# A state-space scan in double steps: first states by copies, evictions moved, and two additions given to TensorE

## The chip, the cores and the metric

The kernel runs on one core of one Trainium2 chip. The metric is the device time of one execution in microseconds (us), taken as the median of several runs. Three runs of the kernel before took 3832.01, 3835.03 and 3840.7 us. A profile is one further execution, with its own time. Its engines are called PE (TensorE's matmuls; PEld its weight loads), DVE (VectorE), ACT (ScalarE), POOL (GpSimd) and SP (SyncE, which issues most DMAs).

## What is computed

Four residual layers on an input of 3 images, 256 channels and 48 x 48 points, each `x = x + layer(groupnorm(x))`: an attention block, two convolutions, and a state-space scan. Only the last layer is touched by the change. Cut to what matters, for a sequence of 2304 points:

```python
xn = (xf - mean(xf)) * rsqrt(var(xf) + 1e-5) * norm_w + norm_b   # over 256 channels
x_in, z = split(xn @ in_proj_w.T)                                # 512 channels each
u = silu(causal_conv4(x_in) + conv_b)
dt_raw, B, C = split(u @ x_proj_w.T)                             # 16, 16, 16
dt = softplus(dt_raw @ dt_proj_w.T + dt_proj_b)                  # 512 channels
h = h * exp(dt * A) + dt * B * u                                 # 512 x 16 states, point by point
y = sum_n(h * C) + u * D
out = (y * silu(z)) @ out_proj_w.T
```

## The kernel before, in words

The first three layers fill the first 2,200 us or so; they are the same in both kernels. The scan layer (from line 995) cuts each image into 6 chunks of 384 points (`CH`), 18 chunks in all, taken one after the other. The 512 channels are four groups `m` of 128, and the 16 states of a channel four groups `g` of 4. A step `s = (chunk, m, g)` covers 128 channels times 4 states times 384 points. It is laid out as 128 partitions (32 channels times 4 states) by 4 rows `q` of 384 points, in a tile `hs`. There are 16 steps a chunk, 288 in all, and `j = 4m + g` numbers them in the chunk. A step consists of:

- `fill` (L1285): `hs = dt*u*B`. DVE multiplies rows 0 and 1 (L1291; the factor comes from PSUM, where PE spread it in `spread_pe`, L1268), POOL rows 2 and 3 (L1292; the factor comes by DMA, `spread`, L1258). The fill of step s+1 is written ahead of step s's scans.
- `decay` (L1296): ACT writes `exp(dt*A)` of one row into one of three PSUM tiles `ps_da` (L1304), three rows ahead of the scan.
- four scans on DVE (L1360), one for each row, along the 384 points. The first state is the constant 0 in an image's first chunk, else a column of `hst`, a pointer to 128 values, which ACT copied from the chunk before (L1372).
- the product with C on POOL (L1375), into `hc`.
- `add_states` (L1309), two steps later: PE adds the states, four small matmuls (L1320), into `ps_y`, in the first step of an `m` behind a diagonal matmul for `u*D` (L1316).
- `gate` (L1325): DVE multiplies the finished `ps_y` by silu(z) (L1327), six steps after the first step of its `m`.

`hs` has four buffers and `hc` three. All other work of the layer is written into the same steps from three lists (`plan`, `after`, `gating`): each entry has a `j`, a place and a chunk relative to the running one. MID is after the second scan of the step, LATE after its product, PE_ after LATE and `add_states`. So chunk k+2 gets its group norm and layer norm (group_scale, two `channel_mean`s on PE, `centre`, `inverse_root`, `normalise`, `tokens`), and chunk k+1 its convolution (`taps`, four times 16 matmul instructions), `take_u`, silu, `project_u`, `take_dbc`, `project_dt`, `softplus`, `take_dt` and `project_z`. The chunk before gets `project_y` and `store`. A silu needs an ACT table of its own and loads the old one again behind it. All these use one PSUM tile `bank` of two banks in turn, so the next user of a bank waits for the last reader.

The order in which lines are written is the order on each of PE, DVE, ACT and POOL: `keep_order` (L1397) chains every instruction to the one before it on its engine. An instruction that waits therefore holds up all that are written after it on the same engine. SP's queue takes its DMAs in the written order as well.

Of the kernel before, what the change touches and what calls it, by code (L numbers as in the profile page):

```python
# [9 lines left out]
F32 = mybir.dt.float32  # L10
I32 = mybir.dt.int32
AF = mybir.ActivationFunctionType
ALU = mybir.AluOpType
# [69 lines left out]
def net(  # L83
# [908 lines left out]

    with ExitStack() as l3:
        wp = l3.enter_context(tc.tile_pool(name="w3", bufs=1))
        act = l3.enter_context(tc.tile_pool(name="act", bufs=2))
        scn = l3.enter_context(tc.tile_pool(name="scn", bufs=2))
        psd = l3.enter_context(tc.tile_pool(name="psd", bufs=3, space=PSUM))
        psr = l3.enter_context(tc.tile_pool(name="psr", bufs=1, space=PSUM))  # L1000
        psg = l3.enter_context(tc.tile_pool(name="psg", bufs=1, space=PSUM))
        psy = l3.enter_context(tc.tile_pool(name="psy", bufs=1, space=PSUM))
# [32 lines left out]
            )  # L1035
        fold = rep[:, 0, :]

        diag = wp.tile([P, DI, P], F32, name="diag")
        for m in range(DI):
            nc.vector.tensor_scalar(diag[:, m, :], ident, v("D", m), None, ALU.mult)  # L1040
# [23 lines left out]
                    bias=sh[:, ct : ct + 1], scale=sc[:, ct : ct + 1],  # L1064
                )

        def channel_mean(src, j):
            for ct in range(CT):
                nc.tensor.matmul(  # L1069
                    bank[:, j, :CH], mean2, src[:, ct, :], start=ct == 0, stop=ct == CT - 1  # L1070
                )

        def centre(k):
            mu = bank[:, 0, :CH].unsqueeze(1).broadcast_to([P, CT, CH])
            nc.vector.tensor_tensor(k.xg, k.xg, mu, ALU.subtract)
            k.sq = act.tile([P, CT, CH], F32, name="sq", bufs=1)
            nc.scalar.activation(k.sq, k.xg, AF.Square)

# [23 lines left out]
        def taps(k, m, lo, hi):  # L1102
            for tap in range(lo, hi):
                for ct in range(CT):
                    nc.tensor.matmul(  # L1105
                        bank[:, m % 2, :CH], wtap[:, tap, ct, m * P : (m + 1) * P],
                        k.xn[:, ct, tap : tap + CH],
                        start=tap == 0 and ct == 0, stop=tap == DCONV - 1 and ct == CT - 1,
                    )

        def take_u(k, m):
            nc.scalar.activation(  # L1112
                k.u[:, m, :], bank[:, m % 2, :CH], AF.Identity, bias=v("conv_b", m)
            )
# [46 lines left out]
        def take_dt(k, m0):  # L1161
            both, pdt = k.dt[:, m0 : m0 + 2, :], bank[:, :, :CH]
            nc.vector.scalar_tensor_tensor(pdt, pdt, 0.0, both, ALU.max, ALU.add)
            nc.vector.tensor_tensor(
                k.dtu[:, m0 : m0 + 2, :], pdt, k.u[:, m0 : m0 + 2, :], ALU.mult
            )
            nc.scalar.copy(both, pdt)  # L1167
            if m0 == 2:
                k.dtd = dram.tile([P, DI, CH], F32, name="dtd")
                nc.sync.dma_start(k.dtd, k.dt)  # L1170
                k.dtud = dram.tile([P // 2, DI, CH], F32, name="dtud")
                nc.sync.dma_start(k.dtud, k.dtu[P // 2 :])
# [13 lines left out]
        def project_y(k, mo):  # L1186
            for m in range(DI):
                nc.tensor.matmul(  # L1188
                    bank[:, mo, :CH], w("out", m * 256 + mo * P, P), k.sz[:, m, :],
                    start=m == 0, stop=m == DI - 1,  # L1190
                )

        def residual(k):
            k.ot = act.tile([P, CT, CH], F32, name="ot")
            nc.sync.dma_start(k.ot, xd[k.b][:, :, k.c * CH : (k.c + 1) * CH])

        def store(k, mo):
            o = k.ot[:, mo, :]
            nc.vector.tensor_tensor(o, bank[:, mo, :CH], o, ALU.add)  # L1199
            nc.sync.dma_start(  # L1200
                out[k.b, mo * P : (mo + 1) * P, k.c * CH : (k.c + 1) * CH], o
            )

        MID, LATE, PE_ = range(3)
        plan = [
            (12, MID, 2, group_scale),
            (12, PE_, 2, lambda k: channel_mean(k.xg, 0)),
            (13, MID, 2, centre),  # L1210
            (13, PE_, 2, lambda k: channel_mean(k.sq, 1)),
            (14, MID, 2, inverse_root),
            (14, LATE, 2, normalise),
            (15, MID, 2, tokens),
            (0, PE_, 1, lambda k: taps(k, 0, 0, 4)),
            (1, LATE, 1, lambda k: take_u(k, 0)),
            (1, PE_, 1, lambda k: taps(k, 1, 0, 4)),
            (3, MID, 1, lambda k: take_u(k, 1)),
            (3, PE_, 1, lambda k: taps(k, 2, 0, 4)),
            (4, PE_, 1, lambda k: taps(k, 3, 0, 4)),  # L1220
# [3 lines left out]
            (7, PE_, 1, project_u),  # L1224
            (8, LATE, 1, take_dbc),
            (8, PE_, 1, lambda k: project_dt(k, 0)),
            (9, MID, 1, lambda k: softplus(k, 0)),
            (10, MID, 1, lambda k: take_dt(k, 0)),
            (10, PE_, 1, lambda k: project_dt(k, 2)),
            (11, MID, 1, lambda k: softplus(k, 2)),  # L1230
            (12, MID, 1, lambda k: take_dt(k, 2)),
        ]

        after = [
# [2 lines left out]
            (4, MID, -1, residual),  # L1237
            (6, PE_, -1, lambda k: project_y(k, 0)),
            (6, PE_, -1, lambda k: project_y(k, 1)),
            (7, LATE, -1, lambda k: store(k, 0)),  # L1240
            (7, LATE, -1, lambda k: store(k, 1)),
        ]

        gating = [
# [32 lines left out]
            k.ps = t  # L1277


        steps = [(at, m, g) for at in range(len(todo)) for m in range(DI) for g in range(4)]  # L1280
        chunks = {}
        tiles = {}
        state = {}

        def fill(s):  # L1285

            at, m, g = steps[s]
            k = chunks[at]
            bb = k.bc[0][:, g, :].unsqueeze(1).broadcast_to([P, 2, CH])
            hs = tiles[s] = scn.tile([P, 4, CH], F32, name="hs", bufs=4)  # L1290
            nc.vector.tensor_tensor(hs[:, 0:2, :], k.ps[:, :, :CH], bb, ALU.mult)  # L1291
            nc.gpsimd.tensor_tensor(hs[:, 2:4, :], k.rows[m][1], bb, ALU.mult)  # L1292

        decays = []

        def decay(n):  # L1296

            s, q = divmod(n, 4)
            if s >= len(steps):
                return  # L1300
            at, m, g = steps[s]
            da = psd.tile([P, 512], F32, tag="d", name="ps_da")
            col = (m * 4 + g) * 4 + q
            nc.scalar.activation(  # L1304
                da[:, :CH], chunks[at].rows[m][0][:, q, :], AF.Exp, scale=amat[:, col : col + 1]
            )
            decays.append(da)

        def add_states(s):  # L1309

            at, m, g = steps[s]
            k = chunks[at]
            hc = tiles.pop(s)
            if g == 0:
                k.y_ps = psy.tile([P, 512], F32, name="ps_y")
                nc.tensor.matmul(  # L1316
                    k.y_ps[:, :CH], diag[:, m, :], k.u[:, m, :], start=True, stop=False
                )
            for q in range(4):
                nc.tensor.matmul(  # L1320
                    k.y_ps[32 * q : 32 * q + 32, :CH], fold, hc[:, q, :],
                    start=False, stop=g == 3,
                )

        def gate(at, m):  # L1325
            k = chunks[at]
# [9 lines left out]
            stage(k)  # L1336
        k.rows = {0: spread(k, 0)}
        spread_pe(k, 0)
        fill(0)
        for n in range(3):  # L1340
            decay(n)
# [3 lines left out]
        for _, _, _, stage in gating:  # L1345
            stage(k)

        for s, (at, m, g) in enumerate(steps):
            k = chunks[at]
            j = 4 * m + g  # L1350
            if j == 2 and at + 2 <= last:
                fetch(at + 2)
            if s + 1 < len(steps):
                fill(s + 1)

            if g == 2 and s + 2 < len(steps):
                spread_pe(chunks[steps[s + 2][0]], steps[s + 2][1])
            hs = tiles[s]
            for q in range(4):
                nc.vector.tensor_tensor_scan(  # L1360
                    hs[:, q, :], decays[q][:, :CH], hs[:, q, :],
                    0.0 if k.c == 0 else state[m, g][:, q : q + 1], ALU.mult, ALU.add,
                )
                decay(4 * s + q + 3)
                if q == 1:
                    if g == 2 and s >= 6:
                        gate(*steps[s - 6][:2])
                    run(at, j, MID)
            del decays[:4]
            if k.c < NCH - 1:  # L1370
                h = state[m, g] = wp.tile([P, 4], F32, name=f"hst{m}{g}")
                nc.scalar.copy(h.unsqueeze(2), hs[:, :, CH - 1 : CH])  # L1372
            cb = k.bc[1][:, g, :].unsqueeze(1).broadcast_to([P, 4, CH])
            hc = tiles[s] = scn.tile([P, 4, CH], F32, name="hc", bufs=3)
            nc.gpsimd.tensor_tensor(hc, hs, cb, ALU.mult)  # L1375
            run(at, j, LATE)
            if s >= 2:
                add_states(s - 2)
            run(at, j, PE_)
            if g == 1 and m + 1 < DI:  # L1380
                k.rows[m + 1] = spread(k, m + 1)
            elif g == 1 and at < last:
                chunks[at + 1].rows = {0: spread(chunks[at + 1], 0)}
        end = len(steps) - 1
        add_states(end - 1)
        add_states(end)
        gate(*steps[end][:2])
        k = chunks[last]
        residual(k)
        for mo in range(2):  # L1390
            project_y(k, mo)
        for mo in range(2):
            store(k, mo)
        keep_order(tc, listed, mark)


# [110 lines left out]
```

## Time and profile before

| | us |
|---|---|
| median of 3 runs | 3835.03 |
| the profiled execution | 3840.89 |
| its span, first to last instruction | 3839.1 |
| PE busy | 3232.1 (84%) |
| DVE busy | 3221.5 (84%) |
| ACT busy | 2228.0 (58%) |
| POOL busy | 1554.8 (40%) |

The shares are over the whole span. POOL works almost only in the scan layer: the page's slices show it at 0 to 3 tenths up to slice 23 and at 9 from there on. Rows of groups read: line, engine, operation, output<-inputs, shapes, count, then busy us and mean ns of one, then the engine's idle us just before them and what ended most of it. A mean can be longer than the pitch at which instructions start, where one begins before the last has ended. Timeline rows read: start and length in us, engine, line, operation, tiles, how many were merged, and in brackets the idle time before and who ended it.

### The profile page before, as it was taken

Reading aid. Unit: us, or ns where it says so; the run is one execution under the profiler, and the core shown is the slowest. Engines: PE = TensorE matmul, PEld = TensorE weight load, DVE = VectorE, ACT = ScalarE, POOL = GpSimd, SP = SyncE. Lnnn points to the kernel's source line nnn. Section 1 sums busy time; section 2 is a strip of 40 time slices with the busy share of each in tenths; the row PEclk is TensorE's granted clock in tenths of the full one; section 3 lists DMA queues with packets and bytes.
Section 4 is the critical chain, followed back from the end, with each engine's and each line's share of the span. In section 5 each row is a group of like instructions: output and inputs, shape, how many; then the busy total and the mean of one; then the engine's idle time right before and its main releaser. Section 6 shows DMA issues by size and latency. Waiting matters only on the chain. (4 is left out here: it accounts for less than half of the span.)

```text
span 3839.1 us, 45642 instructions
## 1 busy us (share of the span) xinstructions
PE 3232.1 (84%) x17010; PEld 1406.6 (37%) x17010; DVE 3221.5 (84%) x3518; ACT 2228.0 (58%) x3216; POOL 1554.8 (40%) x674
## 2 busy tenths in 40 slices
PE   7999999999999988677699757777878878777874
PEld 4323232432323234355577523333333333333331
DVE  4898989779899963799988349999999999999997
ACT  2788787668878762210000147666677666667763
POOL 0000000000000002100000039999999999999998
PEclk9999999999999999888899878888888888888886
DMA  4000000000000015555101133434443433343441
GB/s 170 3 1 1 1 2 1 26 13 1 1 1 2 1 57 173 174 177 177 45 25 42 59 71 100 105 99 104 103 104 91 108 91 99 100 112 92 111 100 34
DMA packets 149962, 266.50 MB, mean 69 GB/s; under 512 B 23441, under 2 KB 123601, under 8 KB 147170
## 3 DMA queue, kind: packets, MB, share of 16 engines
q1 hardware_dynamic: 137634, 245.80, 22.9%
q10 hardware_dynamic: 12096, 17.70, 1.4%
q8 instruction: 135, 2.21, 0.2%
q14 instruction: 97, 0.79, 0.1%
HBM read 216.31 MB, written 46.89 MB: 69 GB/s over the span
## 5 line engine op out<-in xcount | busy, mean ns | idle before, releaser
L587 ACT ACTIVATE pt<-ps_s 128x1024 f32<-128x1024 f32 x972 | 939.0, 1022 | 237.3 <-PE ps_s L583 219.9
L1375 POOL TENSOR_TENSOR hc<-hs,bc 128x1536 f32<-128x1536 f32 x288 | 991.4, 3443 | 85.6 <-DVE hs L1360 56.7
L663 DVE TENSOR_TENSOR part<-part,pt 128x2048 f32<-128x2048 f32 x396 | 906.6, 2289 | 78.4 <-ACT pt L587 53.8
L1360 DVE TENSOR_TENSOR_SCAN hs<-ps_da,hst,hs 128x384 f32<-128x384 f32 x960 | 909.8, 997 | 23.5 <-ACT ps_da L1304 19.9
L1304 ACT ACTIVATE ps_da<-dtr,amat 128x384 f32<-128x384 f32 x1152 | 657.1, 581 | 359.0 <-DVE hs L1360 339.9
L160 POOL TENSOR_TENSOR rstd<-ve,mhalf 128x2 f32<-128x2 f32 (+1 forms) x26 | 17.5, 675 | 1661.7 <-DVE ve L158 1661.7
L583 PE MATMUL ps_s<-q,kt 32*128 32x512 f32 (+1 forms) x4320 | 616.4, 595 | 2.3 <-DVE q L544 0.9
L1292 POOL TENSOR_TENSOR hs<-dtur,bc 128x768 f32<-128x768 f32 x288 | 523.8, 1819 | 77.5 <-DMA dtr<-dtd 77.5
L596 PE MATMUL acc<-pt,vt 128*32 128x512 f32 (+1 forms) x4320 | 523.5, 563 | 8.2 <-DVE o L643 8.0
L927 PE MATMUL ps_c<-vt,u 128*128 128x288 f32 x1728 | 437.8, 417 | 92.9 <-DVE u L257 55.1
L1105 PE MATMUL ps_g<-xn,wtap 128*128 128x384 f32 x1152 | 392.2, 493 | 36.3 <-ACT u L1112 31.3
L927 PEld LDWEIGHTS ps_c<-vt,u 128*128 128x128 f32 x1728 | 335.4, 195 | 190.0 <-issue 56.3
L583 PEld LDWEIGHTS ps_s<-q,kt 32*128 32x128 f32 x4320 | 220.2, 184 | 389.6 <-issue 230.0
L1320 PE MATMUL ps_y<-hc,rep 128*32 128x384 f32 x2304 | 293.5, 596 | 34.6 <-POOL hc L1375 32.7
L1291 DVE TENSOR_TENSOR hs<-ps_r,bc 128x768 f32<-128x768 f32 x288 | 269.1, 934 | 61.8 <-PE ps_r L1273 61.8
L1105 PEld LDWEIGHTS ps_g<-xn,wtap 128*128 128x128 f32 x1152 | 212.7, 189 | 220.1 <-ACT u L1112 54.9
L596 PEld LDWEIGHTS acc<-pt,vt 128*32 128x32 f32 x4320 | 95.7, 108 | 364.3 <-issue 328.5
L943 ACT COPY cb<-ps_c 128x288 f32<-128x288 f32 x48 | 19.0, 395 | 355.5 <-PE ps_c L927 258.5
L1360 DVE TENSOR_TENSOR_SCAN hs<-ps_da,hs 128x384 f32<-128x384 f32 x192 | 170.7, 937 | 17.9 <-ACT ps_da L1304 17.7
L1176 PE MATMUL ps_g<-xn,w3sb 128*128 128x384 f32 x288 | 133.8, 608 | 58.1 <-ACT sz L1184 43.3
L1069 PE MATMUL ps_g<-xg,mean 128*128 128x384 f32 x72 | 52.7, 887 | 105.3 <-ACT dt L1167 78.2
L1320 PEld LDWEIGHTS ps_y<-hc,rep 128*32 128x32 f32 x2304 | 51.3, 118 | 239.1 <-POOL hc L1375 113.5
(204 smaller groups left out, 3265.5 us busy)
## 6 DMA issues: line engine op xcount, KB each, us to landing
wconv<-in_we SPq DMA_DIRECT2D x144, 384.0 KB, 4.3
dtr<-dtd SPq DMA_DIRECT2D x288, 192.0 KB, 3.6
bc<-bcd SPq DMA_DIRECT2D x144, 192.0 KB, 5.9
dtur<-dtud SPq DMA_DIRECT2D x288, 96.0 KB, 2.7
dtd<-dt SPq DMA_DIRECT2D x18, 768.0 KB, 3.5
yc<-ycat ACTq DMA_DIRECT2D x18, 576.0 KB, 5.3
xb<-in_x SPq DMA_DIRECT2D x6, 1152.0 KB, 11.1
ycat<-cur SPq DMA_DIRECT2D x6, 1152.0 KB, 4.9
```

The lines of the kernel that those rows point to most:

```text
L583: nc.tensor.matmul(s[:, j, cols], kt[r, mt * P : (mt + 1) * P], q[r, :n], start=True, stop=True,)
L587: nc.scalar.activation(p[:, h0 : h0 + 2, :], s, AF.Exp)
L596: nc.tensor.matmul(acc[h * HD : (h + 1) * HD, :n], vt[:, mt, g * P + h * HD : g * P + (h + 1) * HD], p[:, h, cols], start=mt == 0, stop=mt ...
L663: nc.vector.tensor_tensor(part, first_p if group == 1 else part, p, ALU.add)
L927: nc.tensor.matmul(pc[:, :HN], u[:, i, dy, ct, m * P : (m + 1) * P], vt[:, i, ct, dy * TW : dy * TW + HN], start=ct == 0 and dy == 0, stop ...
L1105: nc.tensor.matmul(bank[:, m % 2, :CH], wtap[:, tap, ct, m * P : (m + 1) * P], k.xn[:, ct, tap : tap + CH], start=tap == 0 and ct == 0, st ...
L1291: nc.vector.tensor_tensor(hs[:, 0:2, :], k.ps[:, :, :CH], bb, ALU.mult)
L1292: nc.gpsimd.tensor_tensor(hs[:, 2:4, :], k.rows[m][1], bb, ALU.mult)
L1304: nc.scalar.activation(da[:, :CH], chunks[at].rows[m][0][:, q, :], AF.Exp, scale=amat[:, col : col + 1])
L1320: nc.tensor.matmul(k.y_ps[32 * q : 32 * q + 32, :CH], fold, hc[:, q, :], start=False, stop=g == 3,)
L1360: nc.vector.tensor_tensor_scan(hs[:, q, :], decays[q][:, :CH], hs[:, q, :], 0.0 if k.c == 0 else state[m, g][:, q : q + 1], ALU.mult, ALU.add,
L1375: nc.gpsimd.tensor_tensor(hc, hs, cb, ALU.mult)
```

## The change

- A step becomes a double step `(chunk, m, h)`: two groups `g` at once, eight rows of 384 points. There are 8 a chunk, 144 in all, and places `j` 4m+2h and 4m+2h+1 fall in one of them. MID runs after the second and the sixth scan, LATE after the fourth and the eighth, PE_ of an even `j` after the fourth scan, PE_ of an odd `j` at the end, ahead of `add_states`. The latter now belongs to one double step earlier.
- Every row of `hs` gets one more column, its first, with the first state. `first_states` has ACT copy it (8 columns) before the fills of that step are written; `ps_da` has a zero in that column. Every scan now runs over 385 points with the constant 0 as its first state. Scans go over the rows that DVE filled first, then over POOL's.
- Fills and products are one instruction each for a double step (1536 and 3072 elements a partition). `hs` and `hc` have two buffers.
- `take_u` of the first group goes from LATE of 1 to MID of 2, softplus from MID to LATE of 9 and 11. The copy of dt, with the DMAs behind it, is split off `take_dt` as `keep_dt` and goes to LATE of 10 and 12.
- The layer norm's mean is subtracted by PE: `less_mean` multiplies by identity minus mean (4 matmuls for 2), and `centre` becomes an ACT copy out of PSUM, in LATE. The residual is added by PE with an identity matmul in `project_y`, and `store` becomes one ACT copy in place of two DVE additions.

```diff
-        psd = l3.enter_context(tc.tile_pool(name="psd", bufs=3, space=PSUM))
+        psd = l3.enter_context(tc.tile_pool(name="psd", bufs=1, space=PSUM))
...
+        def less_mean(k):
+            for to in range(CT):
+                for ct in range(CT):
+                    nc.tensor.matmul(
+                        bank[:, to, :CH], less[:, int(to != ct), :], k.xg[:, ct, :],
+                        start=ct == 0, stop=ct == CT - 1,
+                    )
...
         def centre(k):
-            mu = bank[:, 0, :CH].unsqueeze(1).broadcast_to([P, CT, CH])
-            nc.vector.tensor_tensor(k.xg, k.xg, mu, ALU.subtract)
+            nc.scalar.copy(k.xg, bank[:, :, :CH])
             k.sq = act.tile([P, CT, CH], F32, name="sq", bufs=1)
             nc.scalar.activation(k.sq, k.xg, AF.Square)
...
-            nc.scalar.copy(both, pdt)
+
+        def keep_dt(k, m0):
+            nc.scalar.copy(k.dt[:, m0 : m0 + 2, :], bank[:, :, :CH])
...
-                    start=m == 0, stop=m == DI - 1,
+                    start=m == 0, stop=False,
                 )
+            nc.tensor.matmul(bank[:, mo, :CH], ident, k.ot[:, mo, :], start=False, stop=True)
...
-            nc.vector.tensor_tensor(o, bank[:, mo, :CH], o, ALU.add)
...
+            nc.scalar.copy(k.ot, bank[:, :, :CH])
...
-            (13, MID, 2, centre),
-            (13, PE_, 2, lambda k: channel_mean(k.sq, 1)),
+            (13, LATE, 2, centre),
+            (13, PE_, 2, square_mean),
...
-            (1, LATE, 1, lambda k: take_u(k, 0)),
             (1, PE_, 1, lambda k: taps(k, 1, 0, 4)),
+            (2, MID, 1, lambda k: take_u(k, 0)),
...
-            (9, MID, 1, lambda k: softplus(k, 0)),
+            (9, LATE, 1, lambda k: softplus(k, 0)),
             (10, MID, 1, lambda k: take_dt(k, 0)),
+            (10, LATE, 1, lambda k: keep_dt(k, 0)),
             (10, PE_, 1, lambda k: project_dt(k, 2)),
-            (11, MID, 1, lambda k: softplus(k, 2)),
+            (11, LATE, 1, lambda k: softplus(k, 2)),
             (12, MID, 1, lambda k: take_dt(k, 2)),
+            (12, LATE, 1, lambda k: keep_dt(k, 2)),
...
-        steps = [(at, m, g) for at in range(len(todo)) for m in range(DI) for g in range(4)]
+        steps = [(at, m, h) for at in range(len(todo)) for m in range(DI) for h in range(2)]
...
+        parts_of_step = [(g, q) for a in range(2) for g in range(2) for q in (2 * a, 2 * a + 1)]
+        slots = [psd.tile([P, 512], F32, name=f"ps_da{i}") for i in range(3)]
...
+        def first_states(s):
+            at, m, h = steps[s]
+            src = zero if chunks[at].c == 0 else state[m, h]
+            hs = tiles[s] = scn.tile([P, 2, 4, CH + 1], F32, name="hs")
+            nc.scalar.copy(hs[:, :, :, 0], src.rearrange("p (g q) -> p g q", g=2))
...
+        def scan(s, part):
+            g, q = parts_of_step[part]
+            b = tiles[s][:, g, q, :]
+            nc.vector.tensor_tensor_scan(
+                b, slots[(8 * s + part) % 3][:, : CH + 1], b, 0.0, ALU.mult, ALU.add
+            )
...
+            for part in range(8):
+                j = 4 * m + 2 * h + part // 4
+                scan(s, part)
+                decay(8 * s + part + 3)
+                if part % 4 == 1:
+                    if h == 1 and part == 1 and s >= 3:
+                        gate(*steps[s - 3][:2])
+                    run(at, j, MID)
+                if part % 4 == 3:
+                    run(at, j, LATE)
+                if part == 3:
+                    run(at, j, PE_)
...
             if s + 1 < len(steps):
+                first_states(s + 1)
                 fill(s + 1)
+            last_states(s)
+            times_c(s)
+            run(at, 4 * m + 2 * h + 1, PE_)
+            if s >= 1:
+                add_states(s - 1)
+
+            if h == 0 and s + 2 < len(steps):
                 spread_pe(chunks[steps[s + 2][0]], steps[s + 2][1])
```

## The prediction

> **What bounds the kernel now.** I read the page's engine shares and slices first, then the stretch of the scan layer alone, then its costliest groups, then each engine's timeline.
>
> The busy time of each engine in 1,300 us inside the scan layer (slices 24 to 39 of the page):
>
> ```profile
> core 0: us, PE busy (x) PEld busy (x) DVE busy (x) ACT busy (x) POOL busy (x), PEclk, DMA share, GB/s
> 2400.00:3700.00 1300.00, 1039.12 (x4072) 430.50 (x4072) 1202.12 (x1378) 899.55 (x1612) 1242.19 (x482) 0.85 0.40 100
> ```
>
> POOL is busy 95.6% and DVE 92.5%: two engines are nearly full, and each idles only where it waits for another. How long a chunk takes is seen in one instruction that runs once a chunk, with its first and last start at the end of the row:
>
> ```profile
> L1117 ACT ACTIVATE sz<-sz x18: 1483/1483/1485, 2278.3 to 3751.8; 128x1536 f32<-128x1536 f32 x18
> ```
>
> (3751.8 - 2278.3) / 17 = **86.7 us a chunk**. The groups that fill it:
>
> ```profile
> L1375 POOL TENSOR_TENSOR hc<-hs,bc 128x1536 f32<-128x1536 f32 x288 | 991.4, 3443 | 85.6 <-DVE hs L1360 56.7
> ...
> L1360 DVE TENSOR_TENSOR_SCAN hs<-ps_da,hst,hs 128x384 f32<-128x384 f32 x960 | 909.8, 997 | 23.5 <-ACT ps_da L1304 19.9
> ...
> L1291 DVE TENSOR_TENSOR hs<-ps_r,bc 128x768 f32<-128x768 f32 x288 | 269.1, 934 | 61.8 <-PE ps_r L1273 61.8
> ...
> L1360 DVE TENSOR_TENSOR_SCAN hs<-ps_da,hs 128x384 f32<-128x384 f32 x192 | 170.7, 937 | 17.9 <-ACT ps_da L1304 17.7
> ```
>
> POOL's idle time is put down to DVE's scans; DVE's largest is a wait for PE. POOL's timeline gives pitches, start to start, that durations do not:
>
> ```profile
> 2980.55 3.44 POOL L1375 TENSOR_TENSOR hc<-hs,bc 128x1536 f32<-128x1536 f32 x1 [0.61 <-DVE hs L1360]
> 2983.94 1.83 POOL L1292 TENSOR_TENSOR hs<-dtur,bc 128x768 f32<-128x768 f32 x1
> 2985.72 3.44 POOL L1375 TENSOR_TENSOR hc<-hs,bc 128x1536 f32<-128x1536 f32 x1
> ```
>
> 1536 elements take 3.39 us of POOL, 768 take 1.78: 2.1 ns an element and about 0.17 us an instruction.
>
> **The engines' own work after the change, one chunk of eight double steps.** I write (m,h) for the step.
>
> POOL: products of 3072 elements, 3.39 + 1536 x 2.1 ns = 6.6 us, and fills of 1536, 3.4 us; 8 x 10.0 = 80.0 us against 16 x 5.17 = 82.7. The trace shows no POOL instruction whose rows are 385 apart and start at an odd element. The fill's and the product's different shapes share one slope, so I take that. A gain below it is excluded, as the elements are the same; above, the farthest row is VectorE's: 694 ns for a strided 128x288 update (L955) against 458 for a plain one (L945), a factor of 1.5.
>
> DVE: the scan whose first state is a constant starts every 0.85 to 0.86 us (937 ns of duration, overlapping), the one with a pointer every 0.91. All become constant, with a 385th element of 2 ns: 64 x 0.86 = 55.0. A fill of 1536: 0.84 (pitch of 768) plus 768 x 1.04 ns (from 934 less the 536 of the 128x384 product at L1327) = 1.64, at most twice 0.84; 8 x 1.64 = 13.1. Gates 4 x 0.5, take_dt 2 x 1.85, normalise 0.9: 6.6. The centring (0.93) and two residual adds (1.1) go to ACT. Together **74.7 us** of DVE, against 81 before.
>
> So the work alone asks 80. It does not set the chunk, because waits that had been hidden are put in DVE's way.
>
> **Where DVE will wait.** Before a scan may start, `first_states` of its step must have run on ACT, which works in order. That copy (0.18 us, the row of `hst`) is queued behind every ACT operation of LATE at odd places and behind the three exponentials ahead. From the start of a step's last scan, an undisturbed ACT needs 0.98 (scan ends, signal) + 0.58 (exp) + 0.18 + 0.05 = 1.8 us; DVE needs 0.86 + 1.64 = 2.5. Hidden, with 0.7 to spare. What is added to ACT beyond that stops DVE:
>
> - softplus, now at the end of steps (2,0) and (2,1): 2.48 us (89.4 us of L1157 to L1159 over 36). 4.27 against 2.5: **1.8 twice**. Before, it lay mid-step, under three exponentials of reserve.
> - the second silu in (1,1), and the new eviction behind it. Its ACT timeline, for the other silu:
>
> ```profile
> 2971.34 1.28 ACT L1117 ACT_TABLE_LOAD   x1
> 2972.63 1.48 ACT L1117 ACTIVATE sz<-sz 128x1536 f32<-128x1536 f32 x1
> 2974.13 1.28 ACT L223 ACT_TABLE_LOAD   x1
> 2975.43 1.09 ACT L1304 ACTIVATE ps_da<-dtr,amat 128x384 f32<-128x384 f32 x2
> ```
>
>  Load, silu and load back take 4.09 us, and what follows starts at once. From scan 5's start ACT needs 0.98 + 0.58 + 4.09 + 1.09 (two exps) + 0.80 (store's copy, the 128x768 copy of L1184) + 0.23 = 7.8; DVE needs 3 x 0.86 + 1.64 = 4.2. **3.6.** The Trainium skill's page "ScalarE: Activation LUTs", section "What ACT_TABLE_LOAD costs", speaks harder against this place: 1.28 us for a load and 1.38 of drain at every switch. By that rule the wait would be 6.3 and not 3.6; the row above, with 1.29 us from load to activation, decides.
> - centre, at the end of (3,0), waits for PE. From scan 3: 0.98 + 0.58 + 0.80 (keep_dt) + 3.0 (less_mean, eight instructions at 0.34, the pitch of taps, and a start) + 0.80 (copy) + 0.84 (Square) + 0.23 and signals = 7.3; DVE 5 x 0.86 + 1.64 = 5.9. **1.4.** (Rows of four such instructions last 1.56 or 2.93 us, so less_mean lies between 2.9 and 5.9.)
> - tokens (1.57) and take_z (0.47) in (3,1): **0.7.**
>
> Then PE. Every second step's `add_states` moves behind the PE_ stage of its place; before, it came ahead of it. Gate needs it. PE's timeline:
>
> ```profile
> 3066.87 5.43 PE L1105 MATMUL ps_g<-xn,wtap 128*128 128x384 f32 x16 [1.74 <-ACT u L1112]
> 3072.23 0.85 PE L1320 MATMUL ps_y<-hc,rep 128*32 128x384 f32 x8
> 3073.01 5.43 PE L1105 MATMUL ps_g<-xn,wtap 128*128 128x384 f32 x16
> 3078.37 0.85 PE L1320 MATMUL ps_y<-hc,rep 128*32 128x384 f32 x8
> ```
>
> Here additions of 0.8 us lie between two tap sets of 5.4. After the change both tap sets come first:
>
> - the previous chunk's last gate, in (0,1): from the end of take_z(1) PE runs project_z 2 and 3 (2.85), the additions of (3,0) with their diagonal (2.3), two tap sets (10.7), the additions of (3,1) (1.5): 17.4 with signals. DVE comes there after 1.09 + 0.23 + 8 x 0.86 + 1.64 + 2 x 0.86 = 11.6. **5.9.** The first silu costs (0,1) 2.9 us of exponentials and is hidden behind this wait. If the gate were ready, 2.9 would stand here.
> - the gate in (3,1) stands behind square_mean (1.56), project_z 0 (1.45) and 1.5 of additions, all after Square: 4.65 against DVE's 1.95. **2.7.**
>
> Sum: 3.6 + 3.6 + 1.4 + 0.7 + 5.9 + 2.7 = **17.9 us**. 74.7 + 17.9 = **92.6 us a chunk**, 5.9 over 86.7. POOL does not hold DVE in this: with 10.0 us a step it ends each product before the step after next is filled (narrowest between (1,0) and (2,0), under 1 us). Unpriced, because covered: the first copies for zeros; take_u, half a step later (PE works from the other bank); 36 identity matmuls for the residual (under the silu); the DMAs of dtd and dtud, which leave half a step later and have some 11 us until the first exponential of the next chunk, where write (3.5), read (3.6) and eight issues (0.43 each) need 10.6. That last cover is thin; without it each us late is a us.
>
> **Ends.** Fifteen full chunks: 15 x 5.9 = 89. A longer first step +4, chunk 0 (no gate before it) -0.5, chunk 16 +1, the last chunk on POOL's pace -2.5, the tail (copies, identity) +1.5. The profiled execution took 3840.9 us (span 3839.1): 3840.9 + 92 = 3933. It lies 5.9 over the median of the runs (3835.0), so **3927** for the median.
>
> **Rivals.**
> 1. *The other side: POOL keeps the pace.* If the waits come to under 80.0 - 74.7 = 5.3 us a chunk, they vanish in DVE's slack and POOL sets 80.0: 15 x (80.0 - 86.7) = -100, **3735**. For it: POOL is the fullest engine and its idle time is DVE's fault. Against: the two gate waits alone hold 8.6, and each is a queue order in the code with a measured 5.4 behind it. Break-even with today is 12.0 us of waits; half of my list would do for faster.
> 2. *Some waits overlap*, and 12 remain: no change, **3835**.
> 3. *POOL pays for rows of 385.* Beyond a factor of 92.6/80.0 = 1.16 it sets the chunk; at 1.2, 96 us, **3980**; at 1.5, 120 us, over 4300, far from the nearest rows. The skill's "GPSIMD Engine Reference", section "Performance pitfalls for Q7 kernels", names 50% more only for steps of over 8 bytes between elements, and here they are 4; no run here shows it.
> 4. *Fills wait for the state copies*, as if the interleaved columns collided: 1.64 of each fill comes behind the copy, some 10 us a chunk, **4080**. Against it, disjoint columns of one tile are written here without order: the memset of `xn`, first in the program, comes later than ScalarE's writes beside it:
>
> ```profile
> 3217.75 1.29 ACT L1096 ACTIVATE xn<-xg,vec 128x384 f32<-128x384 f32 x2
> ...
> 3219.20 0.10 POOL L1092 MEMSET xn<- 128x6 f32 x1
> ```
>
> **Numbers.** Forecast 0.65 (own range 3885 to 3975), rival 1 0.19, rival 2 0.06, rival 3 0.07, rival 4 0.03. Rival 1 reaches from 3735, all waits absorbed, to 3825, a part of them; the range 3760 to 4000 holds about half of it and leaves out the rest, rival 4 and the upper half of rival 3, under 0.2 together. Faster 0.20, within 0.2% (about what a measurement of this kernel can tell from no change) 0.05, slower 0.75.
>
> **What would show it.** Chunk pitch of silu 92 to 93; POOL busy near 86%; scan pitch 0.86; product 6.6 us; DVE's idle time before gate (PE ps_y) 8 to 9 us a chunk, before scans (ACT's state copy) 9. Wrong if DVE's idle time is mostly for POOL, if products take over 7 us, or if the gate in (0,1) does not wait.

## The result and the profile after

The changed kernel takes 4041.65 us (median of four runs, 4040.01 to 4043.27), the kernel before 3835.76 us beside it: a ratio of 1.0536, 95% interval 1.0518 to 1.0554. The forecast was 3927 us, so the sign was right and the size was not: 206 us longer against 91, above the range of 3760 to 4000. The profiled execution took 4040.0 us, its span 4038.1 at a granted clock of 0.905.

Read it in the order of the prediction. First the busy time of each engine in the same 1,300 us inside the scan layer:

```profile
core 0: us, PE busy (x) PEld busy (x) DVE busy (x) ACT busy (x) POOL busy (x), PEclk, DMA share, GB/s
2400.00:3700.00 1300.00, 915.43 (x3666) 426.95 (x3666) 985.73 (x1065) 821.23 (x1454) 1006.41 (x212) 0.86 0.36 88
```

No engine is near full any more: POOL fell from 95.6% to 77%, DVE from 92.5% to 76%. So every engine waits, and the question is for whom. The length of a chunk comes from the silu that runs once in each, by its first and last start:

```profile
L1132 ACT ACTIVATE sz<-sz x18: 1483/1484/1487, 2279.0 to 3953.4; 128x1536 f32<-128x1536 f32 x18
```

(3953.4 - 2279.0) / 17 = 98.5 us, against 86.7. Taken from first scan to first scan over chunks 1 to 15, the fifteen full ones, it is 99.0 against 86.9; that count, and these chunks, are used from here on. The page's groups say what DVE and POOL stood for (busy and mean ns of one, then idle time before them and its releaser):

```profile
L1352 DVE TENSOR_TENSOR_SCAN hs<-ps_da,hs 128x385 f32<-128x385 f32 x1152 | 1005.6, 938 | 283.5 <-ACT hs L1328 264.9
...
L1360 POOL TENSOR_TENSOR hc<-hs,bc 128x3072 f32<-128x3072 f32 x144 | 886.8, 6159 | 334.4 <-DVE hs L1352 317.0
...
L1315 DVE TENSOR_TENSOR hs<-ps_r,bc 128x1536 f32<-128x1536 f32 x144 | 249.5, 1733 | 0.0
...
L1384 DVE TENSOR_TENSOR sz<-ps_y,sz 128x384 f32<-128x384 f32 x72 | 39.2, 544 | 134.5 <-PE ps_y L1377 134.5
```

POOL waits 317 us for DVE's scans; DVE waits 264.9 us for ACT's copy of first states (L1328) and 134.5 us for PE's additions (L1377). The ring ends at the orders of ACT and PE. Sorting DVE's idle time by the step in which it falls gives, for one chunk in us (mean of chunks 1 to 15; the first scan of any step waits 0.1 us for its fill, also the one behind tokens):

| where DVE waits | for | forecast | measured |
|---|---|---|---|
| (0,1), gate | PE, additions behind two tap sets | 5.9 | 5.4 |
| first scan of (1,1) | ACT's copy, behind take_u(2) | none | **6.0** |
| first scan of (2,0) | ACT's copy, behind silu(u) and store | 3.6 | 3.3 |
| behind the two softplus | ACT's copy | 3.6 | 3.6 |
| behind centre | ACT's copy | 1.4 | 2.8 |
| (3,1), gate | PE, additions behind project_z | 2.7 | 2.5 |
| behind tokens and take_z | ACT's copy | 0.7 | 0.1 |
| first scans, for their own fill | DVE | none | 0.2 |
| sum of the waits | | 17.9 | 23.9 |
| DVE's own work | | 74.7 | 75.1 |

One row is missing from the forecast. This is that place on PE, first start and duration of each group, and in brackets the idle time before it and its releaser:

```profile
3058.30 10.59 PE L1120 MATMUL ps_g<-xn,wtap 128*128 128x384 f32 x32
3068.82 1.50 PE L1377 MATMUL ps_y<-hc,rep 128*32 128x384 f32 x16
...
3075.53 7.68 PE L1120 MATMUL ps_g<-xn,wtap 128*128 128x384 f32 x16 [4.36 <-ACT u L1127]
...
3085.20 5.43 PE L1120 MATMUL ps_g<-xn,wtap 128*128 128x384 f32 x16
```

The first row is taps(0) and taps(1) back to back, then the additions that the gate waited for, then taps(2) and taps(3). ACT in the same stretch; its three rows of L1127 here are take_u(0), (1) and (2):

```profile
3069.80 0.58 ACT L1127 ACTIVATE u<-ps_g,vec 128x384 f32<-128x384 f32 x1
...
3074.91 0.56 ACT L1127 ACTIVATE u<-ps_g,vec 128x384 f32<-128x384 f32 x1
...
3090.67 0.58 ACT L1127 ACTIVATE u<-ps_g,vec 128x384 f32<-128x384 f32 x1 [7.03 <-PE ps_g L1120]
3091.15 1.08 ACT L1344 ACTIVATE ps_da<-dtr,amat 128x384 f32<-128x384 f32 x2
3092.16 0.19 ACT L1328 COPY hs<-hst 128x8 f32<-128x8 f32 x1
```

And DVE:

```profile
3070.39 0.56 DVE L1384 TENSOR_TENSOR sz<-ps_y,sz 128x384 f32<-128x384 f32 x1 [5.37 <-PE ps_y L1377]
...
3084.64 1.73 DVE L1315 TENSOR_TENSOR hs<-ps_r,bc 128x1536 f32<-128x1536 f32 x1
3092.39 1.81 DVE L1352 TENSOR_TENSOR_SCAN hs<-ps_da,hs 128x385 f32<-128x385 f32 x2 [6.01 <-ACT hs L1328]
```

Read the three together, in time. The gate holds DVE for 5.37 us; scans, exponentials and take_u(1) behind them on ACT come late by as much (3074.91). PE stands idle for 4.36 us and starts taps(2) (3075.53) only when take_u(1) is through (3074.91 + 0.56 = 3075.47), although taps(2) writes bank 0 and take_u(1) reads bank 1. taps(2) then lasts 7.68 us instead of 5.43. take_u(2) reads bank 0, ready at 3083.2, but starts at 3090.67, when taps(3) has ended its last write to bank 1 (3085.20 + 5.43 = 3090.63). ACT stands for 7.03 us, and the two exponentials written last in step (1,0) and the 0.19 us copy that all of step (1,1) needs are queued behind take_u(2).

### The profile page after: what moved, and what is told of

Same layout as the page of the kernel before. It is cut to its first block, busy times and chain, and to the rows that moved or that the text cites. A ratio compares the mean times of both kernels' runs of the same rounds, so it can differ in the third digit from the quotient of the medians.

```text
span 4038.1 us, 45616 instructions
## 1 busy us (share of the span) xinstructions
PE 3234.2 (80%) x17154; PEld 1473.8 (36%) x17154; DVE 3128.7 (77%) x3326; ACT 2267.7 (56%) x3276; POOL 1442.1 (36%) x386
## 5 line engine op out<-in xcount | busy, mean ns | idle before, releaser
L1352 DVE TENSOR_TENSOR_SCAN hs<-ps_da,hs 128x385 f32<-128x385 f32 x1152 | 1005.6, 938 | 283.5 <-ACT hs L1328 264.9
L1360 POOL TENSOR_TENSOR hc<-hs,bc 128x3072 f32<-128x3072 f32 x144 | 886.8, 6159 | 334.4 <-DVE hs L1352 317.0
L1319 POOL TENSOR_TENSOR hs<-dtur,bc 128x1536 f32<-128x1536 f32 x144 | 495.1, 3438 | 133.8 <-DMA dtr<-dtd 77.0
L1120 PE MATMUL ps_g<-xn,wtap 128*128 128x384 f32 x1152 | 425.1, 529 | 78.1 <-ACT u L1127 74.2
L1120 PEld LDWEIGHTS ps_g<-xn,wtap 128*128 128x128 f32 x1152 | 232.8, 206 | 270.7 <-ACT u L1127 85.3
L1377 PE MATMUL ps_y<-hc,rep 128*32 128x384 f32 x2304 | 236.1, 532 | 34.1 <-POOL hc L1360 30.8
L1315 DVE TENSOR_TENSOR hs<-ps_r,bc 128x1536 f32<-128x1536 f32 x144 | 249.5, 1733 | 0.0
L1164 PE MATMUL ps_g<-dbc,dtsb 17*128 17x384 f32 x144 | 80.6, 695 | 138.0 <-ACT dt L1184 137.3
L1078 PE MATMUL ps_g<-xg,less 128*128 128x384 f32 x144 | 83.7, 751 | 120.8 <-ACT dt L1184 93.5
L1384 DVE TENSOR_TENSOR sz<-ps_y,sz 128x384 f32<-128x384 f32 x72 | 39.2, 544 | 134.5 <-PE ps_y L1377 134.5
## 6 DMA issues: line engine op xcount, KB each, us to landing
xb<-in_x SPq DMA_DIRECT2D x6, 1152.0 KB, 11.1
```

Source lines behind the costliest of these rows:

```text
L1120: nc.tensor.matmul(bank[:, m % 2, :CH], wtap[:, tap, ct, m * P : (m + 1) * P], k.xn[:, ct, tap : tap + CH], start=tap == 0 and ct == 0, st ...
L1315: nc.vector.tensor_tensor(hs[:, :, 0:2, 1:], k.ps[:, :, :CH].unsqueeze(1).broadcast_to([P, 2, 2, CH]), bb, ALU.mult,)
L1319: nc.gpsimd.tensor_tensor(hs[:, :, 2:4, 1:], k.rows[m][1].unsqueeze(1).broadcast_to([P, 2, 2, CH]), bb, ALU.mult,)
L1352: nc.vector.tensor_tensor_scan(b, slots[(8 * s + part) % 3][:, : CH + 1], b, 0.0, ALU.mult, ALU.add)
L1360: nc.gpsimd.tensor_tensor(hc, tiles[s][:, :, :, 1:], cb.broadcast_to([P, 2, 4, CH]), ALU.mult)
L1377: nc.tensor.matmul(k.y_ps[32 * q : 32 * q + 32, :CH], fold, hc[:, g, q, :], start=False, stop=h == 1 and g == 1,)
```

## The theories

**Theory A:** the chunk is set by waits that orders of queues make, and the missed 6.0 us come from a wait kept on the tile `bank` as a whole and not on each of its two banks. Undoing single orders must then take away single waits. **Rival B:** the double step itself is too coarse, so that a wait taken away comes back in the next place. **Rival C:** the layer norm on PE and ACT costs more than it saves DVE. For the 6.0 us itself, **rival D:** take_u(1) comes too late, and the tile has no part in it.

## Experiments

Each is the changed kernel with one edit, if not said otherwise. Ratios are to the kernel before, with their 95% intervals.

**two_tiles.** The tile becomes two tiles of one bank each, and every operation that spans both banks (in centre, softplus, take_dt, keep_dt, the last take_z and store) is split in two, one for each tile.

```diff
-        bank = psg.tile([P, 2, 512], F32, name="ps_g")
+        bank = [psg.tile([P, 512], F32, name=f"ps_g{j}") for j in range(2)]
...
-                        bank[:, m % 2, :CH], wtap[:, tap, ct, m * P : (m + 1) * P],
+                        bank[m % 2][:, :CH], wtap[:, tap, ct, m * P : (m + 1) * P],
...
```

> The changed kernel with PSUM tile bank as two tiles of one bank each; operations over both banks become two. Theory: in the changed kernel taps(2) waits for take_u(1), and take_u(2) for taps(3), only because both are in one tile, though in other banks; that holds ACT, and behind it the state copy, 6.0 us a chunk in step (1,0). Apart, taps(2) starts right after take_u(0) and take_u(2) after taps(2): DVE's idle time there goes from 6.0 to under 0.5, against 1 to 2 us for the extra instructions. Chunk pitch 99.0 to 94 to 95, time about 3965. Rival: PE's slow matmuls after its idle time (7.7 us a tap set) are the cause; then the wait shrinks by 2.3 at most, pitch 97 to 98, time over 4010.

3976.34 us, 1.037 (1.034 to 1.040); 95.5 us a chunk, where 94 to 95 was expected and 97 to 98 if the slow taps alone were the cause. No order was changed, only what a wait is kept on (and some operations are two halves), and DVE's wait at (1,1) went from 6.0 to 0.1 us. On PE, taps(2) now follows at once, at its full pace:

```profile
3134.07 1.50 PE L1384 MATMUL ps_y<-hc,rep 128*32 128x384 f32 x16
3135.49 0.91 PE L1299 MATMUL ps_r<-dtu,rep 32*128 32x384 f32 x4
3136.34 5.43 PE L1121 MATMUL ps_g<-xn,wtap 128*128 128x384 f32 x16
```

That is what A says. Of the 6.0 us, 2.5 came back: the gate of (0,1) now waits 6.8 instead of 5.4, the first scan of (2,1) 2.2 instead of 1.6, with small changes elsewhere.

**u1_early.** The tile as it was, but take_u(1) is issued with take_u(0), so that on ACT it no longer stands behind exponentials that wait for the scans behind the gate.

```diff
             (2, MID, 1, lambda k: take_u(k, 0)),
-            (3, MID, 1, lambda k: take_u(k, 1)),
+            (2, MID, 1, lambda k: take_u(k, 1)),
```

> The changed kernel with take_u(1) straight behind take_u(0), at MID of 2 in place of MID of 3; one tile still. Theory: taps(2) starts 4.6 us earlier, right behind a busy PE, and ends 6.9 us earlier; taps(3) ends before ACT reaches take_u(2). The 6.0 us go, pitch 99.0 to 93.0, time about 3940. Rival (double steps cost through coarser work on ACT or DVE whatever the order): no change, 99.

3983.26 us, 1.0388 (1.0358 to 1.0418); 95.6 us a chunk where 93.0 was expected. The 6.0 are gone here too, and PE does not stop between the tap sets:

```profile
3128.67 10.59 PE L1120 MATMUL ps_g<-xn,wtap 128*128 128x384 f32 x32
...
3141.46 5.43 PE L1120 MATMUL ps_g<-xn,wtap 128*128 128x384 f32 x16
...
3148.89 5.43 PE L1120 MATMUL ps_g<-xn,wtap 128*128 128x384 f32 x16
```

2.5 us came back: 1.2 at the gate of (0,1), 0.8 behind centre, 0.5 for exponentials in the first step. That part is as B forecasts. So D is half true: the lateness and the tile are both needed, and either edit ends the wait.

**adds_first.** The additions again come ahead of the PE_ stage.

```diff
-            run(at, 4 * m + 2 * h + 1, PE_)
             if s >= 1:
                 add_states(s - 1)
+            run(at, 4 * m + 2 * h + 1, PE_)
```

> The changed kernel with add_states ahead of the PE_ stage at the end of a step, as in the kernel before. Theory: gate's two waits for PE, 5.4 and 2.3 us, go; in the first of them the silu's 2.9 us of missing exponentials appear instead. Pitch 99.0 - 4.8 = 94.2, time about 3960. Rival: the gate's wait is covered by another chain of equal length (ACT's silu and evictions), pitch 97 or more.

3906.03 us, 1.0187 (1.0157 to 1.0216); 90.6 us a chunk, 3.6 better than expected, the largest gain of a single edit. DVE's groups in the window 2300 to 3700:

```profile
L1352 DVE TENSOR_TENSOR_SCAN hs<-ps_da,hs 128x385 f32<-128x385 f32 x990 | 865.4, 937 | 231.0 <-ACT hs L1328 179.0 <-ACT ps_da L1344 46.9 <-DVE hs L1315 0.5
...
L1384 DVE TENSOR_TENSOR sz<-ps_y,sz 128x384 f32<-128x384 f32 x61 | 32.4, 532 | 0.2 <-PE ps_y L1377 0.2
```

Both gate waits are gone (0.2 us in all). In their place the exponentials behind the first silu, which the prediction priced at 2.9 as the next in line, cost 3.1. And the wait at (1,1) fell from 6.0 to 1.5, though the tile and take_u stayed as they were: without the gate's wait take_u(1) is hardly late, and PE waits for it 0.23 us there in place of 4.36. The expectation had counted the two waits as separate; they are one chain.

**states_first.** The copy of the next step's first states is issued ahead of the LATE stage, after the eighth scan.

```diff
                     run(at, j, MID)
+                if part == 7 and s + 1 < len(steps):
+                    first_states(s + 1)
...
             if s + 1 < len(steps):
-                first_states(s + 1)
                 fill(s + 1)
```

> The changed kernel with first_states of the next step written ahead of the LATE stage behind the eighth scan. Theory: the copy no longer waits behind softplus (1.6 and 2.0 us), store (0.8 of 3.3) and centre (2.6), but of centre's 2.6 nothing is gained, since gate in the next step waits for PE's square_mean all the same. Pitch 99.0 - 4.4 = 94.6, time about 3970. Rival: the exponentials are what DVE would wait for next, the wait only changes its name, pitch 98 or more.

3986.09 us, 1.0396 (1.0365 to 1.0426); 95.6 us a chunk. DVE's waits behind softplus and centre (6.4 us in all) fell to 0.1 each, as expected, and the gate of (3,1) took part of it back, 2.5 to 5.2:

```profile
L1352 DVE TENSOR_TENSOR_SCAN hs<-ps_da,hs 128x385 f32<-128x385 f32 x936 | 817.8, 937 | 136.6 <-ACT hs L1328 124.6 <-ACT ps_da L1344 2.6 <-DVE hs L1315 0.5
...
L1384 DVE TENSOR_TENSOR sz<-ps_y,sz 128x384 f32<-128x384 f32 x59 | 32.1, 545 | 162.0 <-PE ps_y L1377 162.0
```

**pointer.** Another way to take the copy out of the chain: no copies of first states; each scan takes its first state by a pointer, over 384 points, as in the kernel before.

```diff
-            src = zero if chunks[at].c == 0 else state[m, h]
-            hs = tiles[s] = scn.tile([P, 2, 4, CH + 1], F32, name="hs")
-            nc.scalar.copy(hs[:, :, :, 0], src.rearrange("p (g q) -> p g q", g=2))
+            tiles[s] = scn.tile([P, 2, 4, CH + 1], F32, name="hs")
...
-            b = tiles[s][:, g, q, :]
+            b = tiles[s][:, g, q, 1:]
+            first = 0.0 if chunks[at].c == 0 else state[m, h][:, 4 * g + q : 4 * g + q + 1]
             nc.vector.tensor_tensor_scan(
-                b, slots[(8 * s + part) % 3][:, : CH + 1], b, 0.0, ALU.mult, ALU.add
+                b, slots[(8 * s + part) % 3][:, 1 : CH + 1], b, first, ALU.mult, ALU.add
```

> The changed kernel without the copies of first states: scans run over 384 points and take the first state by pointer, as before; double steps and all orders as changed. Theory: the copy is what carries ACT's delays to DVE at a step's start. Without it the exponentials ahead cover softplus and centre wholly and the rest in part: waits of 6.0, 3.3, 1.6, 2.0 and 2.6 become 4.3, 1.2, 0, 0 and 0; gate in (3,1) grows to 4.9; scans cost 2.9 more. 99.0 becomes about 94, time 3960. Rival: the doubling itself is to blame, and the pitch rises by the 2.9 of the pointers to 102.

3985.33 us, 1.0386 (1.0363 to 1.0409); 95.6 us a chunk, where about 94 was expected. No scan waits for a copy now. Step (1,1) still waits, one scan later and less: 3.6 us for an exponential queued behind take_u(2), in place of 6.0; in (2,0) exponentials cost 2.1. The gates wait 5.0 and 5.2. The scans start every 0.905 us again instead of 0.856, 3 us more a chunk, and DVE's own work rises to 78.7. The copies do save what they were said to save; their place in ACT's queue costs more (DVE waits 16.9 us a chunk here, 23.9 with them).

**three.** The edits of u1_early, adds_first and states_first together.

> The changed kernel with all three orders mended: take_u(1) behind take_u(0), add_states ahead of PE_ at a step's end, first_states ahead of the LATE stage. Theory: what remains of DVE's waits is the two silus (3.1 and 2.6 us) and the layer norm's chain in (3,1), some 2; 75.0 + 8 = 83 us a chunk, POOL's own pace 8 x (6.24 + 3.41) = 77.2 not yet reached. Time about 3785, faster than before. Rival: the waits of the single runs hide one another and the next chain (PE) takes over at 87 or more: no gain over before.

3835.32 us, 0.9989 (0.9979 to 1.0000): the time of the kernel before. 86.5 us a chunk, 3.5 more than expected. DVE works 75.3 us a chunk against 80.3 before and waits 11.1 against 6.5. Nearly all that the change saves on DVE is still given back, now for the exponentials behind the first silu (3.7), the copy behind store (2.6) and, in (3,1), take_z ahead of normalise (2.4).

**three_mid.** As three, but the copies go ahead of the MID stage, after the sixth scan, so that the second silu and store no longer stand before them.

```diff
                 decay(8 * s + part + 3)
+                if part == 5 and s + 1 < len(steps):
+                    first_states(s + 1)
                 if part % 4 == 1:
```

> As three, but first_states already ahead of the MID stage behind the sixth scan, so ahead of the second silu too. Theory: the silu's 2.6 us fall to about 1.1 (what is then missing are exponentials), pitch 81.5, time about 3760. Rival: the copy now comes before POOL's product two steps back has ended (6.2 us after the scans, where the sixth scan comes 6.1 us after them), ACT waits there with the exponentials behind it, and the pitch is 84 or more.

3815.50 us, 0.9933 (0.9917 to 0.9950): 0.7% faster than the kernel before. 85.25 us a chunk instead of 81.5. The engines' busy time, columns as in the first fence above, and then DVE's scans in the window 2300 to 3700:

```profile
2400.00:3700.00 1300.00, 1043.42 (x4256) 477.17 (x4258) 1154.08 (x1238) 932.93 (x1689) 1170.06 (x248) 0.88 0.41 102
```

```profile
L1352 DVE TENSOR_TENSOR_SCAN hs<-ps_da,hs 128x385 f32<-128x385 f32 x1052 | 923.9, 939 | 90.6 <-ACT ps_da L1344 76.9
```

No scan waits for a copy any more; what scans still wait for are exponentials, 3.7 us at the first silu and 1.1 at the second. In (3,1) normalise waits 2.4 us and the gate 1.6. ACT never waits for POOL's product in the window 2400 to 3700, so the rival's mechanism did not come, though the pitch is the one that it named. POOL is 90% busy; at its own pace (8 x (6.235 + 3.41), pitches of product and fill) a chunk would take 77.2 us. DVE works 75.6 us a chunk and waits 9.7.

**three_late.** As three_mid, and inverse_root, take_z, normalise and tokens half a step later, so that normalise finds take_z done.

```diff
-            (14, MID, 2, inverse_root),
-            (14, LATE, 2, normalise),
-            (15, MID, 2, tokens),
+            (14, LATE, 2, inverse_root),
+            (15, MID, 2, normalise),
+            (15, LATE, 2, tokens),
...
-            (14, MID, 1, lambda k: take_z(k, 0, 0)),
+            (14, LATE, 1, lambda k: take_z(k, 0, 0)),
```

> As three_mid, with inverse_root and take_z(0) half a step later (LATE of 14), normalise at MID of 15 and tokens at LATE of 15. Theory: normalise's wait of 2.2 us in (3,1) goes, nothing else changes: pitch 85.25 to about 83.3, time about 3785, still over POOL's 77.2. Rival: tokens then comes too late for taps(0), gate's wait in (0,1) returns, and the pitch stays at 85 or over.

3819.16 us, 0.9952 (0.9936 to 0.9967); 85.4 us a chunk, no better than three_mid. Normalise still waits 2.4 us, now for PE and ACT, and the gate of (0,1) 1.3 in place of 0.1. The wait moved, as the rival said.

**tensor_only.** The kernel before with only the layer norm's mean and the residual on PE and their evictions on ACT.

```diff
         def centre(k):
-            mu = bank[:, 0, :CH].unsqueeze(1).broadcast_to([P, CT, CH])
-            nc.vector.tensor_tensor(k.xg, k.xg, mu, ALU.subtract)
+            nc.scalar.copy(k.xg, bank[:, :, :CH])
...
-        def store(k, mo):
-            o = k.ot[:, mo, :]
-            nc.vector.tensor_tensor(o, bank[:, mo, :CH], o, ALU.add)
...
+        def store(k):
+            nc.scalar.copy(k.ot, bank[:, :, :CH])
...
```

> The kernel before with one part of the change alone: layer norm's mean and the residual by TensorE, with the evictions as ACT copies at the old places. Theory: DVE loses 2.0 us of work a chunk, but centre's copy now holds ACT until less_mean's eight instructions are done, and POOL is near its own pace: within 1 us of 86.9 a chunk, 3820 to 3850. Rival: DVE's relief counts fully, 84.9, about 3800.

3868.66 us, 1.0075 (1.0058 to 1.0092); 88.3 us a chunk, 1.4 over the kernel before where at most 1 was expected. DVE's own work falls by 1.6 us (80.3 to 78.8), and its waits rise from 6.5 to 9.5. The waits of DVE's scans for exponentials in the window 2400 to 3700 (us in all, times, longest), which were 23.2 us, 22 times, in the kernel before:

```profile
DVE hs L1369 <- ACT ps_da L1313: 75.7, 68, 1.9
```

What DVE saves comes back, about doubled, as waits for ACT's exponentials. That speaks for C, in that kernel.

**no_tensor.** The changed kernel with this part taken back to DVE.

```diff
         def centre(k):
-            nc.scalar.copy(k.xg, bank[:, :, :CH])
+            mu = bank[:, 0, :CH].unsqueeze(1).broadcast_to([P, CT, CH])
+            nc.vector.tensor_tensor(k.xg, k.xg, mu, ALU.subtract)
...
-            nc.scalar.copy(k.ot, bank[:, :, :CH])
             for mo in range(CT):
+                o = k.ot[:, mo, :]
+                nc.vector.tensor_tensor(o, bank[:, mo, :CH], o, ALU.add)
```

> The changed kernel with layer norm's mean and the residual on VectorE again (subtraction at LATE of 13, two additions at LATE of 7). Theory: ACT is rid of two copies and PE of four matmuls in the chain behind (3,0); the waits for the state copy there and behind the second silu shrink by 2.8, gate's in (3,1) by 0.6, against 2.0 of DVE work: 97.6, about 4018. Rival: that part is what the change gains by, and without it the pitch is over 100.5.

4066.72 us, 1.059 (1.0569 to 1.0611); 100.8 us a chunk, 1.8 more than the changed kernel where 1.4 less was expected. DVE then does 77.2 us of its own work and waits 23.6, almost as long as in the changed kernel (23.9), in other places: store's additions wait 2.0 for PE, the gate of (0,1) 6.5, that of (3,1) 3.5. C falls for the changed kernel. Alone on the kernel before, the layer norm and residual part costs 1.4 us a chunk; all the rest of the change without it costs 13.9, both together 12.1.

## Why the prediction was right and wrong

**Right:** slower, and by the mechanism named: DVE's own work falls (74.7 us a chunk expected, 75.1 measured), POOL falls far from full, and DVE waits at every place listed but the one behind tokens, on the engine named, to within 1.4 us. Scans start every 0.856 us (0.86 expected), so the copies do their work; a fill of 1536 took 1.73 us. None of the rivals came: POOL does not hold DVE, rows of 385 cost it nothing (rival 3), fills did not wait for the copies (rival 4). The thin cover of the dtd and dtud DMAs held in that no DVE time went to it: POOL's fills wait for the reads of dtud 25.4 us in the whole scan layer, and once, for 77.0 us, for those of dtd, ahead of the first fill of all.

**Wrong, the step that failed:** "Unpriced, because covered: the first copies for zeros; take_u, half a step later (PE works from the other bank)". PE doesn't work from the other bank while ACT reads this one: the wait is kept on the tile, and both banks are one tile. The take_u that the change moved is the first; the waits came at take_u(1) and take_u(2), which kept their places but rest on the same premise. This could be read in the trace of before. Its PE row of taps(2), after take_u(1) (2979.12 to 2979.68, bank 1):

```profile
2979.73 5.43 PE L1105 MATMUL ps_g<-xn,wtap 128*128 128x384 f32 x16 [1.74 <-ACT u L1112]
...
2985.87 5.43 PE L1105 MATMUL ps_g<-xn,wtap 128*128 128x384 f32 x16
```

and its ACT row of take_u(2), which reads bank 0:

```profile
2991.34 0.58 ACT L1112 ACTIVATE u<-ps_g,vec 128x384 f32<-128x384 f32 x1 [3.17 <-PE ps_g L1105]
```

Bank 0 was ready at 2985.16 (2979.73 + 5.43); ACT started after taps(3) ended in bank 1 (2985.87 + 5.43 = 2991.30). The bracket of 1.74 even stands in a fence of the prediction, on another chunk's row, and was read past. The wait already reached DVE there, through the exponentials that stand behind take_u(2):

```profile
2991.82 1.08 ACT L1304 ACTIVATE ps_da<-dtr,amat 128x384 f32<-128x384 f32 x2
...
2992.43 1.02 DVE L1360 TENSOR_TENSOR_SCAN hs<-ps_da,hst,hs 128x384 f32<-128x384 f32 x1 [1.29 <-ACT ps_da L1304]
```

On average that scan waits 1.4 us a chunk. It was no more because exponentials run three scans ahead, and no copy that the next step needs stood behind take_u. The Trainium skill's page "PSUM — Partial Sum Buffer", section "PSUM bank collisions raise a hardware error", asks to guard PSUM by bank (and quadrant); by that alone neither wait would be needed. The rows of taps(2) and take_u(2) show this program waiting for more than that, and two_tiles ends it.

What it costs in the changed kernel is 6.0 us a chunk at (1,1). The miss in the span is (4038.1 - 3839.1) - 92 = 107 us. Of this, 15 full chunks make 93 (12.1 us longer each, 5.9 forecast), and chunks 0 and 16, which have the same place, 15 (8.4 and 7.4 us longer; -0.5 and +1 forecast); start, last chunk and tail together make 1.3 less than forecast. Against the 92.6 us of the sum, a chunk of 99.0 is 6.4 too long: 6.0 in waits, which the row of (1,1) makes up by itself while the other rows balance, and 0.4 in DVE's work.

**Smaller misses.** The scan behind centre waits 2.8 us and not 1.4: `less_mean` took 4.6 us where 3.0 was taken, inside the stated bounds of 2.9 to 5.9. The product of 3072 elements starts its successor after 6.24 us and not 6.6; "A gain below it is excluded, as the elements are the same" was wrong: the second 1536 elements cost 1.85 ns each, not 2.1. Why was not tried. POOL busy was expected near 86% and is 77%, from this and from the longer chunk. The 0.7 us behind tokens and take_z did not come. Taken by what DVE waits for, the state copies cost 15.7 us a chunk where 9 was said, and the gates 7.8 where 8 to 9 was.

**What stays open.** A is shown for the loss: moving take_u(1), the additions and the copies takes 99.0 us a chunk to 85.25, 1.6 under the kernel before. What B forecasts came in part: two_tiles, u1_early and states_first lost 2.5 to 3.7 us again of the waits that they ended, and three_mid is 8 us from POOL's pace. That the length of the double step is the reason is not shown. Whether two_tiles on top of three_mid, two_tiles in the kernel before, or the silus in another place would come nearer was not tried.

## What to carry to other kernels

When work is moved later in an in-order queue, its cost is not its own duration but the wait of whatever short, urgent instruction stands behind it: here the place of one copy of 0.19 us decided 3.4 us a chunk. Before calling a step covered by a second buffer, look in the old trace whether any instruction on one half has ever started while the other half was still in use; a bracket of idle time there, however cheap today, is tomorrow's wait. And two waits in one chain are not two terms of a sum: taking away the first (adds_first) took most of the second with it.

## What the hardware showed that was not expected

- **PE is slow after it has stood idle.** The same 16 instructions of taps(2) took 7.68 us after 4.36 us of idle time and 5.43 when PE was kept busy (u1_early, two_tiles). The granted clock shows it: 0.50 in the first 4.0 us of the slow set (3075.5 to 3079.5), 1.00 during taps(3) (3085.2 to 3090.6). The four of `project_dt` took 2.92 us after 7.75 us of idle time and 1.55 otherwise. This agrees in kind with the Trainium skill's page "TensorE: Matmul & The Clock Gate", section "Part 1: The HAM clock gate", by which an idle window of about 3.4 us halves the clock until about 3.4 us of work have passed. Here the slow start costs 2.25 us on top of the wait, rather more than the 1.7 us that 3.4 us at half the clock would add, an estimate from that page. The length of the idle time alone does not settle it in this trace: four instructions of `project_z` took 2.93 us at a clock of 0.50 after only 2.40 us of idle time (1.45 otherwise), while eight of `project_u` took 2.82 us at a clock of 1.00 after 2.50. Why the first were slow stays open.
- **A scan straight behind its own fill waits for the fill's end.** From fill to first scan 1.84 us pass, where the prediction took 1.64 from pitches; the fill itself lasts 1.73, and every step shows the 0.1 us of idle time behind it.
- **POOL's products grow by less than their elements:** 3.39 us from start to start for 1536 in the kernel before, 6.24 for 3072.
